# Vision-tower kernel: the tokenizer's last group in a hand-written order, and keys and values with their transposes one group ahead

## The chip, the cores and the metric

The kernel runs on one core of one Trainium2 chip. The metric is the device time of one launch in microseconds, as the median of several runs. A core has a matrix engine (TensorE, PE in the profile; its weight loads are shown as PEld), a vector engine (VectorE, DVE), a scalar engine (ScalarE, ACT), GpSimd (POOL) and a queue engine that issues transfers (SyncE, SP). Each engine works through its own list of instructions in order and waits for the others through semaphores.

## The reference

A small vision tower on four images of 3 x 224 x 224, all in 32-bit floats. The part that matters here is the tokenizer and the beginning of the attention of layer 0:

```
patches = 8 x 8 patches of x, 784 rows of 192 for each image
tokens  = layernorm(layernorm(patches) @ W1 + b1)
tokens  = concatenate([tokens, tokens, tokens], axis=1)
h       = silu(layernorm(tokens @ Wp1 + bp1)) @ Wp2 + bp2
# layer 0
m   = layernorm(layernorm(h) , gamma, beta)
q, k, v = m @ Wq, m @ Wk, m @ Wv
att = softmax over the images t of sum(q[s] * k[t]) per head
h   = h + (att applied to v, gated by sigmoid(m @ Wg + bg)) @ Wo + bo
h   = h + mixture of six experts, two for each row
# layer 1: linear attention, then a shared MLP and four experts, two for each row
```

The three copies of the tokens are equal, so the kernel computes one of them and writes each output row three times.

## The kernel before, in words

The 3136 rows (four images of 784) are cut into 28 tiles of 112 rows, and these into **seven groups of four tiles** (`groups`, `GT = 4`, `GN = 448` rows). The array `h` stays in SBUF for the whole kernel.

The tokenizer works by groups. For group g, `first_rows` (L506) multiplies the patches by a combined weight into PSUM (`pw`, L515), takes mean and variance of one half on VectorE (L519, L520), adds a correction (L522), takes a square root on ScalarE (L523) and its reciprocal on VectorE (L524). It then scales the other half (L528), takes its statistics (L531, L532), a second square root (L534) and reciprocal (L535), and writes the normalised rows `xn` (L538). `turned_rows` (L544) transposes `xn` on TensorE (in the helper `transposed`, L264) and applies Silu on ScalarE (L548) into `xTt`. The last part of `tokenize` (L566) multiplies `xTt` by `Wp2` (`pwp`, in the helper `mm_rows`, L284) and adds the bias into `h`. `tokenize(g)` does the first part for group g, the second for g - 1 and the third for g - 2. Up to the seventh group (g = 6) the planner of the framework decides how these instructions are interleaved on each engine.

From there on the order is written out by hand: inside `tc.manual_schedule` TensorE, VectorE and ScalarE execute in the order in which the program names the instructions. `tokenize(7)` and `tokenize(8)`, the leftovers of groups 5 and 6, stand in this part.

For keys and values, `second_norm(g)` takes the statistics of `h` (L236, L237) and works out the scale of two layer norms in a row, with two square roots on ScalarE (L239, L245). `second_rows(g)` writes the rows (L1060). `keys_values(g)` (L1065) transposes them, scales them on ScalarE into `mT` (L1070), multiplies by `Wk` and `Wv` (`pkv`, L273) and copies the products to `kq` and `vT` (L1079); in between it does `second_norm` and `second_rows` of group g + 1. At last it adds `bo` to `h` (L1087). After some of the groups come the products of queries and keys on VectorE (`products`, L739), and the first product with `headmask` (`pl`, L746) begins the attention proper.

Silu and square root need different function tables on ScalarE; a change from one to the other is an instruction of its own (ACT_TABLE_LOAD).

SP meanwhile fills two DRAM arrays, `xrows` and `yrows`, with zeros from the tile `nothing` (L468 to L473), in blocks of eight times 128 rows. Rows are scattered into `xrows` by GpSimd later (L950).

Of the kernel before, what the change touches and what calls it, by code (L numbers as in the profile page):

```python
# [27 lines left out]
P = 128  # L28
TT = 112
# [31 lines left out]
def tile_vit_tower(ctx: ExitStack, tc: tile.TileContext, a: dict, out: bass.AP):  # L61
# [168 lines left out]
    def ln_stats(src, n, twice=False):  # L230


        st = small.tile([TT, GT, 6], F32, tag="st", name="st")
        mv = small.tile([TT, GT, 2], F32, tag="mv", name="mv")
        for j in range(n):
            nc.vector.bn_stats(st[:, j, :], src(j))  # L236
            nc.vector.bn_aggr(mv[:, j, :], st[:, j, :])  # L237
        r = small.tile([TT, GT], F32, tag="rstd", name="rstd")
        nc.scalar.activation(r[:, :n], mv[:, :n, 1], AF.Sqrt, bias=eps[:TT])  # L239
        nc.vector.reciprocal(r[:, :n], r[:, :n])  # L240
        if twice:
# [27 lines left out]
    def mm_t(n, w, wcols, xT, name, chunks=2):  # L269

        pm = ps_tile(name)
        for c in range(chunks):
            nc.tensor.matmul(  # L273
                pm[: wcols.stop - wcols.start, :n], w[:, c, wcols], xT(c),
                start=(c == 0), stop=(c == chunks - 1),
            )
        return pm[: wcols.stop - wcols.start, :n]

    def mm_rows(tiles, xT, w, name, chunks=2):

        pm = ps_tile(name)[:TT].rearrange("p (t d) -> p t d", t=2)
        for i, t in enumerate(tiles):
            for c in range(chunks):
                nc.tensor.matmul(  # L284
                    pm[:, i, :], xT(c, t), w[:, c, :], start=(c == 0), stop=(c == chunks - 1)
                )
# [10 lines left out]
    def cut(t0, n):  # L297
        return slice(t0 * TT, (t0 + n) * TT)
# [166 lines left out]
        nc.tensor.transpose(pc[:, :nrows], stage, ident[:nrows, :nrows])  # L465
        turned = nc.vector.tensor_copy(cols, pc[:, :nrows])

    nothing = tokp.tile([P, 8 * D], F32, tag="nothing", name="nothing")  # L468
    nc.gpsimd.memset(nothing, 0.0)
    for r in range(0, XROWS, 8 * P):  # L470
        n = min(8, (XROWS - r) // P)
        for rows_ in (xrows, yrows):
            put = nc.sync.dma_start(  # L473
                out=rows_[r : r + n * P, :].rearrange("(p k) d -> p (k d)", k=n),
                in_=nothing[:, : n * D],
            )
# [27 lines left out]


    def first_rows(g):  # L506

        t0 = groups[g][0]
        y = tokp.tile([TT, GT, D], F32, tag="y", name="y", bufs=2)
        st = small.tile([TT, GT, 6], F32, tag="st", name="st")  # L510
        mv = small.tile([TT, GT, 2], F32, tag="mv", name="mv")
        for j in range(GT):
            pm = ps_tile("pw1")[:TT]
            for c in range(2):
                nc.tensor.matmul(  # L515
                    pm, pTf[:, c, cut(t0 + j, 1)], Wall[:, c, :], start=(c == 0), stop=(c == 1)
                )
# [5 lines left out]
        nc.scalar.activation(r, r, AF.Sqrt, bias=zero[:TT])  # L523
# [12 lines left out]
        xn = tokw.tile([TT, GT, D], F32, tag="xn", name="xn")  # L536
        for j in range(GT):
            nc.vector.tensor_scalar(  # L538
                xn[:, j, :], y[:, j, :], mv[:, j, 0:1], r[:, j : j + 1],
                ALU.subtract, ALU.mult,  # L540
            )
        return xn

    def turned_rows(xn):  # L544
        xT = tokw.tile([P, 2, GN], F32, tag="xTt", name="xTt")
# [10 lines left out]

    def tokenize(g):
        if g < len(groups):
            normed[g] = first_rows(g)
        if 1 <= g <= len(groups):  # L560
            third[g - 1] = turned_rows(normed.pop(g - 1))
        if g >= 2:
            sT = third.pop(g - 2)
            t2 = groups[g - 2][0]
            for two in halves(range(GT)):
                nc.vector.tensor_tensor(  # L566
                    h[:, t2 + two[0] : t2 + two[0] + 2, :],
                    mm_rows(two, lambda c, j: sT[:, c, cut(j, 1)], Wp2, "pwp2"),
                    over(bp2, 2), ALU.add,
                )  # L570
# [120 lines left out]
    ENG = mybir.EngineType  # L691
    by_hand = {ENG.DVE, ENG.PE, ENG.Activation}
    qTs, gates, atts, oTs, sums, rows0, turned0, logits0, picked, mixed = ({} for _ in range(10))
    pqs, pgs = {}, {}
    scatters = []
# [350 lines left out]
        nc.vector.tensor_tensor(wk[:, 1, t0 : t0 + n], second, first, ALU.mult)  # L1046


    xns = {}

    def second_norm(g):
        t0 = groups[g][0]
        return ln_stats(lambda j: h[:, t0 + j, :], GT, twice=True)

    def second_rows(g, stats):
        mv, r = stats
        t0 = groups[g][0]
        xn = xns[g] = tokw.tile([TT, GT, D], F32, tag="xn", name="xn")
        for j in range(GT):
            nc.vector.tensor_scalar(  # L1060
                xn[:, j, :], h[:, t0 + j, :], mv[:, j, 0:1], r[:, j : j + 1],
                ALU.subtract, ALU.mult,
            )

    def keys_values(g):  # L1065
        t0 = groups[g][0]
        at = cut(t0, GT)

        def put(c, pt):
            nc.scalar.activation(  # L1070
                mT[:, c, at], pt, AF.Identity, scale=col("gamma", c), bias=col("beta", c)
            )

        transposed(xns.pop(g), GT, put)
        if g + 1 < len(groups):
            stats = second_norm(g + 1)
        for w, dst in ((Wk, kT), (Wv, vT)):
            for o in range(2):
                nc.scalar.copy(  # L1079
                    dst[:, o, at],  # L1080
                    mm_t(GN, w, slice(o * P, (o + 1) * P), lambda c: mT[:, c, at], "pkv"),
                )
            if dst is kT and g + 1 < len(groups):
                second_rows(g + 1, stats)

        ht = h[:, t0 : t0 + GT, :]
# [816 lines left out]
```

## Time and profile before

| what | us |
|---|---|
| median of three runs | 787.35 (786.73 to 787.98) |
| the profiled execution, its own time | 833.42 |
| its span in the trace | 831.6 |
| TensorE busy in it | 744.5 |
| VectorE busy in it | 501.5 |
| ScalarE busy in it | 333.6 |
| GpSimd busy in it | 130.7 |

The profiled execution took longer than the runs without a profile. Durations below are from the profiled execution; differences are taken against its time, and carried over to the median. In the profile L12 is line 12 of the kernel, `out<-in` names the tiles, and `x8` counts instruction records; a 32-bit matrix product leaves two records. Ends of TensorE's records are modelled, so its starts are the better guide.

### The profile page before, as it was taken

What the parts mean: (1) busy time and instruction counts of PE and PEld (TensorE: products, weight loads), DVE (VectorE), ACT (ScalarE), POOL (GpSimd) and SP (SyncE); (2) the same over time, 40 slices, a digit from 0 to 9 for tenths busy, and PEclk for the clock granted to TensorE, in tenths of its full rate; (3) what the DMA queues carried; (4) which work ended last, traced back from release to release, by engine and by line L of the source; (5) the groups of instructions that cost most, each with busy time, mean ns of one, the idle gap of its engine ahead of it and who ended that gap; (6) DMA issues with size and microseconds to landing.
All of it is one profiled execution on the core that took longest, in us unless ns stands there. A gap on an engine that the chain in (4) does not pass through costs nothing.

```text
span 831.6 us, 10856 instructions
## 1 busy us (share of the span) xinstructions
PE 744.5 (90%) x3516; PEld 502.6 (60%) x3516; DVE 501.5 (60%) x1549; ACT 333.6 (40%) x789; POOL 130.7 (16%) x219
## 2 busy tenths in 40 slices
PE   7899969998987886999999997179999999999996
PEld 4655545555654564888878873155777685555553
DVE  4677775867878724355447565269994735555441
ACT  1567763556375732342223325114564503222221
POOL 5200000000256155300020206532000000000000
PEclk9999989999899888899999998669999999999998
DMA  8499994000012933232342342211000002333333
GB/s 208 147 420 417 421 418 206 1 2 0 20 59 62 368 93 117 86 113 88 96 128 89 112 125 86 78 45 33 2 1 0 1 4 64 95 96 99 95 99 92
DMA packets 58182, 97.38 MB, mean 117 GB/s; under 512 B 14519, under 2 KB 48494, under 8 KB 53262
## 3 DMA queue, kind: packets, MB, share of 16 engines
q1 hardware_dynamic: 50832, 80.52, 28.0%
q0 software_dynamic: 6112, 14.01, 5.8%
q10 hardware_dynamic: 1182, 2.16, 1.0%
q8 instruction: 28, 0.46, 0.2%
q14 instruction: 28, 0.23, 0.1%
HBM read 30.93 MB, written 65.74 MB: 116 GB/s over the span
## 4 chain that ended last, share of the span: by engine, by line
PE 73%; DVE 9%; ACT 6%; another core or an unknown queue 4%; issue 3%; DMA 2%; SPq 1%; POOL 0%; DVEq 0%; ACTq 0%; POOLq 0%
PE pb L1224 11%; PE pw L515 6%; PE pyb L1241 5%; PE pkv L273 5%; PE pe L273 5%; PE pqk L1625 4%; PE ps L273 4%; PE pt L264 3%; PE pwp L284 3%; PE pout L1740 3%; PE pout L1745 3%; PE ps L1857 3%; PE pukx L1699 3%; PE ps L1851 2%
## 5 line engine op out<-in xcount | busy, mean ns | idle before, releaser
L950 POOL DMA_INDIRECT xrows<-xn,pos x56 | 59.1, 1055 | 260.1 <-ACT kq L714 207.3
L1420 POOL DMA_INDIRECT ys<-yrows,pos x56 | 53.9, 962 | 167.0 <-DMA yrows<-yb 135.2
L1224 PE MATMUL pb<-xTb,own 128*128 128x256 f32 x240 | 60.7, 398 | 6.5 <-ACT xTb L1214 3.6
L1241 PE MATMUL pyb<-own,hb 128*128 128x256 f32 x240 | 58.4, 386 | 2.7 <-ACT hb L1230 2.4
L1230 ACT ACTIVATE hb<-pb,own 128x256 f32<-128x256 f32 x74 | 34.8, 475 | 63.0 <-PE pb L1224 42.0
L1224 PE MATMUL pb<-hb,own 128*128 128x256 f32 x240 | 58.7, 387 | 0.3 <-DVE hb L1232 0.3
L1224 PEld LDWEIGHTS pb<-xTb,own 128*128 128x128 f32 x240 | 45.6, 199 | 16.2 <-ACT xTb L1214 4.4
L1247 DVE TENSOR_TENSOR yb<-pyb,eb 128x512 f32<-128x512 f32 x30 | 20.7, 691 | 55.2 <-PE pyb L1241 39.3
L1241 PEld LDWEIGHTS pyb<-own,hb 128*128 128x128 f32 x240 | 45.8, 192 | 10.1 <-ACT hb L1230 3.2
L1625 PE MATMUL pqk<-Wqkv,lxT 128*112 128x512 f32 x112 | 50.0, 595 | 0.7 <-issue 0.5
L515 PE MATMUL pw<-Wall,pT 128*112 128x512 f32 x112 | 49.3, 593 | 0.0
L1224 PEld LDWEIGHTS pb<-hb,own 128*128 128x128 f32 x240 | 44.4, 195 | 6.7 <-DVE hb L1232 0.9
L1699 PE MATMUL pukx<-xa,uk 112*128 112x258 f32 x112 | 29.2, 418 | 18.1 <-ACT uk L1657 18.1
L1214 ACT COPY xTb<-ptb 128x512 f32<-128x512 f32 x30 | 17.5, 584 | 69.0 <-PE ptb L1210 63.7
L273 PE MATMUL pe<-xT,eW 128*128 128x448 f32 x112 | 45.2, 546 | 0.0
L264 PE MATMUL pt<-ident,xn 112*128 112x112 f32 x224 | 34.3, 286 | 11.5 <-DVE xn L538 6.6
L264 PEld LDWEIGHTS pt<-ident,xn 112*128 112x128 f32 x224 | 26.9, 151 | 25.6 <-issue 8.8
L1232 DVE TENSOR_SCALAR hb<-pb,own 128x256 f32<-128x256 f32 x46 | 22.1, 481 | 31.4 <-PE pb L1224 28.8
L1699 PEld LDWEIGHTS pukx<-xa,uk 112*128 112x128 f32 x112 | 22.9, 210 | 22.0 <-issue 18.4
L515 PEld LDWEIGHTS pw<-Wall,pT 128*112 128x112 f32 x112 | 19.6, 177 | 25.1 <-issue 21.4
L739 DVE SCALAR_TENSOR_TENSOR prod<-kq 128x784 f32<-128x784 f32 x32 | 30.3, 969 | 7.1 <-ACT kq L714 5.2
L1625 PEld LDWEIGHTS pqk<-Wqkv,lxT 128*112 128x112 f32 x112 | 19.2, 177 | 25.3 <-issue 24.2
(361 smaller groups left out, 1503.6 us busy)
## 6 DMA issues: line engine op xcount, KB each, us to landing
xrows<-nothing SPq DMA_DIRECT2D x19, 1024.0 KB, 19.6
yrows<-nothing SPq DMA_DIRECT2D x19, 1024.0 KB
out_dram<-h SPq DMA_DIRECT2D x26, 336.0 KB, 3.7
xb<-xrows SPq DMA_DIRECT2D x30, 256.0 KB, 2.8
yrows<-yb SPq DMA_DIRECT2D x30, 256.0 KB, 2.1
ew<-in_L_ffn_expert_w_dram SPq DMA_DIRECT2D x6, 768.0 KB, 11.8
wb<-wd SPq DMA_DIRECT2D x28, 112.0 KB, 3.3
img<-in_x_dram SPq DMA_DIRECT2D x2, 588.0 KB
```

The costliest lines, as they stand in the source:

```text
L264: nc.tensor.transpose(pt[:, j * TT : (j + 1) * TT], xn[:, j, c * P : (c + 1) * P], ident[:TT, :TT])
L273: nc.tensor.matmul(pm[: wcols.stop - wcols.start, :n], w[:, c, wcols], xT(c), start=(c == 0), stop=(c == chunks - 1),)
L284: nc.tensor.matmul(pm[:, i, :], xT(c, t), w[:, c, :], start=(c == 0), stop=(c == chunks - 1))
L515: nc.tensor.matmul(pm, pTf[:, c, cut(t0 + j, 1)], Wall[:, c, :], start=(c == 0), stop=(c == 1))
L739: nc.vector.scalar_tensor_tensor(prod, qTs[s][:, o, :], 1.0, kT[:, o, t * SEQ : (t + 1) * SEQ], ALU.mult, ALU.mult, accum_out=atts[s][:, o ...
L950: put = nc.gpsimd.indirect_dma_start(out=xrows[:, :], out_offset=bass.IndirectOffsetOnAxis(ap=pos[:, k, t0 + j : t0 + j + 1], axis=0), in_ ...
L1224: nc.tensor.matmul(pm, wm[:, c, o * P : (o + 1) * P], src[:, c, :], start=(c == 0), stop=(c == 1),)
L1230: nc.scalar.activation(dst[:, o, :], pm, AF.Relu, bias=b)
L1241: nc.tensor.matmul(pm[:, t, :], src[:, c, t * P : (t + 1) * P], wm[:, c, :], start=(c == 0), stop=(c == 1),)
L1420: got = nc.gpsimd.indirect_dma_start(out=y[:, j, k, :], out_offset=None, in_=yrows[:, :], in_offset=bass.IndirectOffsetOnAxis(ap=pos[:, k, ...
L1625: nc.tensor.matmul(pqk, xT[:, c, cut(j, 1)], Wqkv[:, c, : 2 * D], start=(c == 0), stop=(c == 1),)
L1699: nc.tensor.matmul(pg, uks[u][:, k, c * P : (c + 1) * P], xas[u % 4][:, k, : D + 2], start=(j == 0), stop=(j == TPI - 1),)
```

## The change

1. `first_rows` becomes the generator `first_steps`, with a stop after the first reciprocal and another after the second statistics.
2. The planner's loop covers only groups 0 to 5. Before the last of these, `second_norm(0)` and `second_rows(0)` are done, so the rows of the first keys group are ready early. `xn` gets a third buffer (`bufs=3`) for that.
3. Group 6 is in a hand-written block. Its first step comes before the Silu of group 5; then come the transposes and Silu of group 5, the second step, `last_rows(4)`, and the rest.
4. Keys and values are split. `turn_second(g)` does the transposes and `mT`, `projected` one of the two products with its copies. `keys_values(g)` does the product with `Wk`, the statistics of group g + 2, the transposes of group g + 1, the product with `Wv`, and the rows of group g + 2. In group 0 the transposes and Silu of group 6 stand ahead of those of group 1, and `last_rows(6)` after the product with `Wv`.
5. `nothing` holds seven rows of 256 for each partition in place of eight, so the zeros go out in 46 transfers in place of 40.

```diff
-    nothing = tokp.tile([P, 8 * D], F32, tag="nothing", name="nothing")
+    nothing = tokp.tile([P, 7 * D], F32, tag="nothing", name="nothing")
     nc.gpsimd.memset(nothing, 0.0)
-    for r in range(0, XROWS, 8 * P):
-        n = min(8, (XROWS - r) // P)
+    for r in range(0, XROWS, 7 * P):
+        n = min(7, (XROWS - r) // P)
...
     def first_rows(g):
+        for _ in first_steps(g):
+            pass
+
+    def first_steps(g):
...
         nc.scalar.activation(r, r, AF.Sqrt, bias=zero[:TT])
         nc.vector.reciprocal(r, r)
+        yield
...
             nc.vector.bn_aggr(mv[:, j, :], st[:, j, :])
+        yield
         r = small.tile([TT, GT], F32, tag="rstd", name="rstd")
...
-        xn = tokw.tile([TT, GT, D], F32, tag="xn", name="xn")
+        xn = tokw.tile([TT, GT, D], F32, tag="xn", name="xn", bufs=3)
...
-        return xn
+        normed[g] = xn
...
-    for g in range(len(groups)):
+    n = len(groups)
+    for g in range(n - 1):
+        if g == n - 2:
+            second_rows(0, second_norm(0))
         tokenize(g)
+    ENG = mybir.EngineType
+    by_hand = {ENG.DVE, ENG.PE, ENG.Activation}
+    with tc.manual_schedule(engines=by_hand):
+        steps = first_steps(n - 1)
+        next(steps)
+        third[n - 2] = turned_rows(normed.pop(n - 2))
+        next(steps)
+        last_rows(n - 3)
+        for _ in steps:
+            pass
     tok.close()
...
+    def turn_second(g):
+        if g >= len(groups):
+            return
+        at = cut(groups[g][0], GT)
...
         transposed(xns.pop(g), GT, put)
-        if g + 1 < len(groups):
-            stats = second_norm(g + 1)
-        for w, dst in ((Wk, kT), (Wv, vT)):
-            for o in range(2):
-                nc.scalar.copy(
-                    dst[:, o, at],
-                    mm_t(GN, w, slice(o * P, (o + 1) * P), lambda c: mT[:, c, at], "pkv"),
-                )
-            if dst is kT and g + 1 < len(groups):
-                second_rows(g + 1, stats)
...
+    def keys_values(g):
+        projected(g, Wk, kT)
+        if g + 2 < len(groups):
+            stats = second_norm(g + 2)
+        if g == 0:
+            third[n - 1] = turned_rows(normed.pop(n - 1))
+        turn_second(g + 1)
+        projected(g, Wv, vT)
+        if g == 0:
+            last_rows(n - 1)
+        if g + 2 < len(groups):
+            second_rows(g + 2, stats)
...
     with tc.manual_schedule(engines=by_hand):
-        second_rows(0, second_norm(0))
-        tokenize(len(groups))
+        turn_second(0)
+        last_rows(n - 2)
+        second_rows(1, second_norm(1))
         keys_values(0)
-        tokenize(len(groups) + 1)
         for g in range(1, len(groups)):
             keys_values(g)
```

More of the change, by code (lines that the diff above doesn't have):

```diff
@@ L558, in tokenize @@
         if g < len(groups):
-            normed[g] = first_rows(g)
+            first_rows(g)
         if 1 <= g <= len(groups):
@@ L562, in tokenize, with last_rows, second_norm, second_rows @@
         if g >= 2:
[L563 to L569, printed above, removed]
-                )
-    for g in range(len(groups)):
-        tokenize(g)
+            last_rows(g - 2)
+    def last_rows(g):
+        sT = third.pop(g)
+        t2 = groups[g][0]
+        for two in halves(range(GT)):
+            nc.vector.tensor_tensor(
+                h[:, t2 + two[0] : t2 + two[0] + 2, :],
+                mm_rows(two, lambda c, j: sT[:, c, cut(j, 1)], Wp2, "pwp2"),
+                over(bp2, 2), ALU.add,
+            )
+    xns = {}
+    def second_norm(g):
+        t0 = groups[g][0]
+        return ln_stats(lambda j: h[:, t0 + j, :], GT, twice=True)
+    def second_rows(g, stats):
+        mv, r = stats
+        t0 = groups[g][0]
+        xn = xns[g] = tokw.tile([TT, GT, D], F32, tag="xn", name="xn", bufs=3)
+        for j in range(GT):
+            nc.vector.tensor_scalar(
+                xn[:, j, :], h[:, t0 + j, :], mv[:, j, 0:1], r[:, j : j + 1],
+                ALU.subtract, ALU.mult,
+            )
+    n = len(groups)
+    for g in range(n - 1):
+        if g == n - 2:
+            second_rows(0, second_norm(0))
+        tokenize(g)
+    ENG = mybir.EngineType
[8 more added lines that the diff above has]
+            pass
     tok.close()
@@ L690, in tile_vit_tower @@
     nc.vector.tensor_scalar(bgh, col2("bg"), 0.5, None, ALU.mult)
-    ENG = mybir.EngineType
-    by_hand = {ENG.DVE, ENG.PE, ENG.Activation}
     qTs, gates, atts, oTs, sums, rows0, turned0, logits0, picked, mixed = ({} for _ in range(10))
@@ L1046, in mix3 @@
         nc.vector.tensor_tensor(wk[:, 1, t0 : t0 + n], second, first, ALU.mult)
[L1049 to L1067, printed above, removed]
+    def turn_second(g):
+        if g >= len(groups):
+            return
+        at = cut(groups[g][0], GT)
         def put(c, pt):
@@ L1074, in keys_values, with projected @@
         transposed(xns.pop(g), GT, put)
-        if g + 1 < len(groups):
-            stats = second_norm(g + 1)
-        for w, dst in ((Wk, kT), (Wv, vT)):
-            for o in range(2):
-                nc.scalar.copy(
-                    dst[:, o, at],
-                    mm_t(GN, w, slice(o * P, (o + 1) * P), lambda c: mT[:, c, at], "pkv"),
-                )
-            if dst is kT and g + 1 < len(groups):
-                second_rows(g + 1, stats)
-        ht = h[:, t0 : t0 + GT, :]
+    def projected(g, w, dst):
+        at = cut(groups[g][0], GT)
+        for o in range(2):
+            nc.scalar.copy(
+                dst[:, o, at],
+                mm_t(GN, w, slice(o * P, (o + 1) * P), lambda c: mT[:, c, at], "pkv"),
+            )
+    def keys_values(g):
[10 more added lines that the diff above has]
+            second_rows(g + 2, stats)
+        ht = h[:, groups[g][0] : groups[g][0] + GT, :]
         nc.vector.tensor_tensor(ht, ht, over(bo, GT), ALU.add)
     with tc.manual_schedule(engines=by_hand):
-        second_rows(0, second_norm(0))
-        tokenize(len(groups))
+        turn_second(0)
+        last_rows(n - 2)
+        second_rows(1, second_norm(1))
         keys_values(0)
-        tokenize(len(groups) + 1)
         for g in range(1, len(groups)):
```

## The prediction

> **What bounds the kernel now.** I read the page's busy shares, then the TensorE timeline over 94 to 182 us (the stretch that the edits touch), then the granted clock in narrow windows, then VectorE's and ScalarE's timelines across the one long hole.
>
> ```profile
> PE 744.5 (90%) x3516; PEld 502.6 (60%) x3516; DVE 501.5 (60%) x1549; ACT 333.6 (40%) x789; POOL 130.7 (16%) x219
> ```
>
> TensorE is the bound over the whole, so microseconds in which it waits or runs slowly are what an edit can win. Its timeline (start, us, what; idle time and releaser in brackets):
>
> ```profile
> 93.86 7.03 PE L515 MATMUL pw<-Wall,pT 128*112 128x512 f32 x16
> ...
> 105.05 0.32 PE L577 MATMUL ptable<-ident,table 1*78 1x1 f32 x4
> 111.94 2.07 PE L264 MATMUL pt<-ident,xn 112*128 112x112 f32 x8 [6.57 <-DVE xn L538]
> 113.80 5.33 PE L284 MATMUL pwp<-Wp,xTt 128*112 128x256 f32 x16
> 118.97 0.93 PE L264 MATMUL pt<-ident,xn 112*128 112x112 f32 x8
> 120.33 3.27 PE L273 MATMUL pkv<-mT,Wk 128*128 128x448 f32 x8 [0.43 <-ACT mT L1070]
> 123.44 3.17 PE L273 MATMUL pkv<-mT,Wv 128*128 128x448 f32 x8
> 126.45 3.62 PE L284 MATMUL pwp<-Wp,xTt 128*112 128x256 f32 x16
> ```
>
> After the seventh group's products L515 TensorE runs dry for 6.57 us, waiting for that group's normalised rows (xn, L538). Then the same eight transposes take 2.07 us instead of 0.93, and the same sixteen records of pwp 5.33 instead of 3.62. The windows say why (PEclk is the last column but two):
>
> ```profile
> 105.00:110.00 5.00, 0.37 (x5) 0.23 (x4) 4.84 (x18) 4.19 (x6) 0.00 (x0) 1.00 1.01 419
> 110.00:112.00 2.00, 0.06 (x1) 0.09 (x1) 1.86 (x9) 0.30 (x1) 0.00 (x0) 0.61 1.02 418
> 112.00:114.00 2.00, 2.00 (x9) 1.64 (x10) 1.51 (x8) 0.71 (x2) 0.00 (x0) 0.50 1.04 426
> 114.00:116.00 2.00, 2.00 (x7) 1.42 (x6) 1.38 (x4) 1.99 (x3) 0.00 (x0) 0.50 1.01 414
> 116.00:118.00 2.00, 2.00 (x8) 1.53 (x7) 0.56 (x1) 0.23 (x1) 0.00 (x0) 0.69 1.01 410
> ```
>
> The clock halves at about 110.4 and is back at about 117.2. Why are the rows late? ScalarE stands between:
>
> ```profile
> 103.28 0.72 ACT L548 ACTIVATE xTt<-pt,cols 128x448 f32<-128x448 f32 x1
> 104.03 1.28 ACT L523 ACT_TABLE_LOAD   x1
> 105.32 0.30 ACT L523 ACTIVATE rstd<-rstd,zero 112x4 f32<-112x4 f32 x1
> ```
>
> The square root L523 had its input from VectorE at 102.19 (L522, 102.03 plus 0.16) but stood behind another group's Silu and its table; VectorE's reciprocal L524 came only at 105.77. Later VectorE ran the first keys group's statistics (L236, 109.09 to 111.2) ahead of the reciprocal L535 that the seventh group needs.
>
> [...] The trace agrees: halved 5.0 us after the work stopped at 105.37, restored 5.3 us after it resumed at 111.94. It also shows a harder case: at 206.0 us the clock fell (0.50 over 206.0 to 209.4) though no single wait before it was over 0.99 us; sparse transposes were enough. [...] the trace shows 1.28 us with the square root at once behind it, so I price a switch at 1.28.
>
> **The change, part by part.** W2(g) below is last_rows (pwp), T(g) a group's eight transposes (0.93 us), groups 0 to 6.
>
> *What can be won in this stretch.* The hole 6.57. The seven waits for mT before each Wk product: three of 0.43 and four of 0.48, together 3.21. The cold clock: 2.07 − 0.93 = 1.1 and 5.33 − 3.62 = 1.7, together 2.8. Sum 12.6 us. Matrix products are only reordered, so this is the ceiling.
>
> *Last group by hand, and turned later.* The order is now products L515 of group 6, T(5), W2(4), the table, T(0), W2(5), Wk(0), and only then T(6). Between the products and T(6) lie 0.93 + 3.45 + 0.3 + 0.93 + 3.45 + 3.1 = 12.2 us of TensorE work, where 4.6 us stood before (100.73 to 105.37). The rows came 11.2 us after the products (100.73 to 111.94), so T(6) should not wait. (W2 is 126.45 to 129.90, Wk 120.33 to 123.44, each from start to the next start.) The square root goes ahead of the Silu of T(5), and saves that Silu's tables: the built program has 37 table loads for 39. ScalarE's two loads fewer (2.6 us) are off TensorE's path and priced at nothing beyond the hole.
>
> *second_norm(0) and second_rows(0) moved up, ahead of group 5.* About 3.6 us more for VectorE in a cycle of 11.1 (four statistics with aggregates at 0.42, small steps 0.6, rows 1.3) in which it was idle 2.8 (1.24 + 1.04 + 0.51). It comes out 0.8 late, and since the hand order no longer interleaves, TensorE waits for xn(5) ahead of T(5): bound 0 to 2.5, I take 1.5. Rows arriving 0.34 apart spread the transposes by another 0.7. **A: 2.2 lost.**
>
> *T(1) behind Wk(0).* From the end of W2(5), VectorE must add h (0.75), do the statistics to the rows (130.71 to 134.64 in the trace of group 2: 3.93), and give the first row (0.5): 5.2; TensorE has Wk 3.1 and T(6) 0.93. Wait 1.2, plus 0.4 for xn(6) queued ahead of that add, plus 0.7 of spread. Bounds 0 to 4. **B: 2.3 lost.**
>
> *W2(6) behind Wv(0).* It needs the Silu of T(6). ScalarE holds that behind both square roots of second_norm(2), which VectorE begins only after xn(1). From xn(1)'s first row: other rows 1.0, to the second root 3.19 (130.71 to 133.90), root 0.3, table 1.28, first Silu 0.72, hand-over 0.1: 6.6. TensorE has T(1) 1.6 and Wv 3.1. Bounds 0.5 to 3.5. **C: 1.9 lost.** The mT and vT copies queued behind the Silu fall into later slack.
>
> *Transposes one group ahead.* T(g+1) runs between Wk and Wv, so mT's 1.34 us on ScalarE lies under 3.1 us of Wv: six of the seven waits go, and the first too (T(0) runs before W2(5)). If that cover were gone, 0.45 each would return. VectorE was 77% busy over 140 to 160 (15.39 of 20); with the group's period cut from 7.53 to about 6.9 it becomes 84%, not yet the bound. Allow **D: 0.2**, bounds 0 to 1.5.
>
> *Zeros in blocks of seven.* 46 transfers for 40, the same bytes at 419 GB/s; six more issues at 0.33 us on SP, which waits on landings there anyway. The transfers end near 135, scatters start after 220: nothing, bounds 0 to 0.3. The first kq copy waits for the kernel's first loads in both built programs, not for the zeros still under way then. A third buffer for xn adds no wait.
>
> *Clock afterwards.* A and B are each a wait followed by sparse transposes, like the case at 206.0. [...] After B it mostly falls on Wv and eats wait C, free; after A it costs up to 1.7. Mean 1.0, bounds 0 to 3.4.
>
> **Sum.** 12.6 − (2.2 + 2.3 + 1.9 + 0.2) − 1.0 = **5.0 us** won by the first pl (L746, 180.26). Beyond it all waits are on work of the chain itself, so I pass it on whole. The profiled execution took 833.42 (span 831.6), 46 above the median of 787.35; the chain shows waits of 6.10, 4.88 and 11.09 us on unknown queues at 516 to 540, far from this stretch, so I take 5.0 off the median: **782.3**.
>
> **Rivals.**
> 1. *Smaller gain*: A, B and C nearer their upper bounds and two cold spells. 12.6 − 8 − 2.5 = 2.1: 785.2. For it: the manual order forbids filling a gap with other work.
> 2. *Nothing*: VectorE becomes the bound of the keys; six periods of 6.9 us stretch back to 7.5 (3.6) and B and C grow by 1.4 together: 5.0 − 5.0 = 0, 787.4. Against it: 77% busy.
> 3. *Slower*: the clock stays at half from A through C[...]. Loss is half the cold time. With 6.6 of waits, it decides against the change from (12.6 − 6.6) × 2 = 12 us cold; the stretch from A to W2(6)'s end, some 25 us, would cost 12.5 and give 793.8. Against it: W2(5) with Wk(0) is about 7 us dense, enough for recovery by the trace's 5.3.
> 4. *Not what it says*: the built program shows all moves above, so this is excluded.
>
> **How the numbers follow.** 0.2% is 1.6 us, about what measurement of this kernel can tell from no change. Main case 0.64 (gain 3.4 to 7), rival 1 0.19 (gain 1.6 to 3.4), within 0.2% 0.07, slower 0.10. Faster is 0.83. The likeliest case's range is 780.3 to 784.0; for 8 in 10, with most of rival 1, 779.8 to 786.2.
>
> **What would show it.** Right: no TensorE wait over 2.5 us between 95 and 130; waits of 1 to 2 us ahead of T(5), T(1) and W2(6); no mT wait before Wk; the first pl near 175; clock not at 0.5 for over 7 us. Wrong: a wait on xn(6) at T(6), one over 3 us anywhere, or a cold clock throughout 103 to 128.

## The result and the profile after

The changed kernel took **781.75 us** (median of 4 runs, 780.17 to 781.97) where the kernel before, on the same chip, took 787.29 (4 runs, 786.73 to 787.98): ratio 0.9925, 95% interval 0.9908 to 0.9942, so 5.5 us faster by the medians, and 4.6 to 7.2 by the interval. The forecast was 782.3, range 779.8 to 786.2.

The profiled execution took 781.84 us (span 780.1). The page's busy shares:

```profile
PE 732.4 (94%) x3516; PEld 495.7 (64%) x3516; DVE 500.2 (64%) x1549; ACT 330.5 (42%) x787; POOL 134.4 (17%) x219
```

The execution profiled before took 833.42, far above the 787 of the other runs; profiling isn't the reason, since the one profiled after lies among its runs (780.17 to 781.97), and on the chips of the experiments the kernel before takes 827. TensorE's share rose from 90% to 94%, but most of that is not the change: from the first pl to the end of the span the execution profiled before took 651.3 us and this one 604.9, in code that no edit touches. The wait list over 480 to 580 of the experiment e5 below, which runs the changed kernel on another chip (engine, tile, line, releaser: us in total, times, longest), has the largest of those losses too:

```profile
POOL ys L1455 <- DMA yrows<-yb: 21.9, 1, 21.9
...
PE pukx L1734 <- ACT uk L1692: 18.4, 1, 18.4
```

The profile after shows neither, the profile before shows both (21.8 and 18.1), so it goes with the chip or the execution, not with the kernel; which of the two isn't shown. The two spans must not be subtracted; only the stretch that was edited can be compared. TensorE's timeline of it, after (start, us, what; idle time and releaser in brackets):

```profile
96.36 7.03 PE L519 MATMUL pw<-Wall,pT 128*112 128x512 f32 x16
104.50 1.58 PE L264 MATMUL pt<-ident,xn 112*128 112x112 f32 x8 [1.11 <-DVE xn L544]
...
113.98 3.17 PE L273 MATMUL pkv<-mT,Wk 128*128 128x448 f32 x8
116.99 0.93 PE L264 MATMUL pt<-ident,xn 112*128 112x112 f32 x8
119.65 1.57 PE L264 MATMUL pt<-ident,xn 112*128 112x112 f32 x8 [1.73 <-DVE xn L593]
121.06 4.88 PE L273 MATMUL pkv<-mT,Wv 128*128 128x448 f32 x8
125.96 3.89 PE L284 MATMUL pwp<-Wp,xTt 128*112 128x256 f32 x16
129.69 3.17 PE L273 MATMUL pkv<-mT,Wk 128*128 128x448 f32 x8
132.70 0.93 PE L264 MATMUL pt<-ident,xn 112*128 112x112 f32 x8
133.47 3.19 PE L273 MATMUL pkv<-mT,Wv 128*128 128x448 f32 x8
...
175.22 0.28 PE L784 MATMUL pl<-part,headmask 128*128 128x8 f32 x2
```

The hole of 6.57 us is gone, and the last group's transposes (116.99) follow Wk without a wait. Two waits stand in its place, 1.11 ahead of the sixth group's transposes and 1.73 ahead of the second keys group's. The mT waits are gone: Wk follows pwp, and Wv follows the next group's transposes 0.77 us after their start (132.70 to 133.47). One product is long, Wv at 121.06: 4.88 us for 3.19. The narrow windows (the last columns are the granted clock, the DMA share and GB/s) say why:

```profile
120.00:122.00 2.00, 1.99 (x9) 1.21 (x10) 1.90 (x9) 0.00 (x0) 0.00 (x0) 0.87 1.02 423
122.00:124.00 2.00, 2.00 (x4) 1.01 (x3) 1.17 (x7) 0.71 (x3) 0.00 (x0) 0.50 0.99 409
124.00:126.00 2.00, 1.98 (x5) 0.57 (x3) 0.24 (x2) 1.99 (x3) 0.00 (x0) 0.78 1.05 434
```

The clock is at half (0.50) from about 121.5 to 124.9, 3.4 us, where before it was so for 6.8. ScalarE's timeline shows what Silu of the last group stands behind:

```profile
106.11 0.30 ACT L527 ACTIVATE rstd<-rstd,zero 112x4 f32<-112x4 f32 x1 [2.16 <-DVE rstd L526]
...
107.72 1.34 ACT L554 ACTIVATE xTt<-pt,cols 128x448 f32<-128x448 f32 x2
...
123.57 0.30 ACT L245 ACTIVATE v<-v,eps 112x4 f32<-112x4 f32 x1 [0.64 <-DVE v L244]
...
125.19 1.34 ACT L554 ACTIVATE xTt<-pt,cols 128x448 f32<-128x448 f32 x2
```

The square root L527 now runs as soon as its input is there; the load of Silu's table (1.28 us) and the sixth group's Silu come behind it. The last group's Silu (125.19) runs only after a root of the third keys group (L245, 123.57), and pwp at 125.96 follows it. The wait ahead of that root (0.64) is for VectorE.

**The measure used below.** The totals scatter: on the three chips of the experiments, before took 827.2, 827.1 and 827.5 us with single times from 822 to 834. A trace of the stretch is sharper. I take the time from the start of the fifth group's products (the first record of its sixteen, L515 or L519) to the first pl. Three traces with the stretch as before give 108.6, 108.1 and 107.7 (before, e1 and e11; mean 108.1), by how much of pwp the half clock covers (in before it read 0.50 from 110.4 to 117.3, and pwp starts at 113.80; pwp takes 5.17, 4.61 and 4.25 us from start to start); the changed kernel gives 101.4 in both of its traces (73.84 to 175.22 after, 72.63 to 174.02 in e5). So the stretch won **6.7 us** against the mean, and 7.2 against the one trace of before that the prediction used.

| kernel | stretch, us | less than 108.1 | total, median us | ratio to before, 95% |
|---|---|---|---|---|
| e1 before again | 108.1 | | 830.5 (one run) | |
| e2 keys alone | 105.6 | 2.5 | 822.75 | 0.9953 (0.9927 to 0.9979) |
| e3 tokenizer alone | 102.0 | 6.1 | 818.21 | 0.9895 (0.9864 to 0.9925) |
| e4 Silu first | 105.5 | 2.6 | 823.44 | 0.9956 (0.9933 to 0.9978) |
| e5 the change | 101.4 | 6.7 | 818.42 | 0.9898 (0.9865 to 0.9932) |
| e6 hole kept warm | 106.4 | 1.7 | 822.06 | 0.9942 (0.9920 to 0.9965) |
| e7 both hand-overs | 98.2 | 9.9 | 815.81 | 0.9862 (0.9821 to 0.9904) |
| e8 both, early statistics | 96.4 | 11.7 | 813.05 | 0.9827 (0.9795 to 0.9859) |
| e9 Silu ahead | 100.9 | 7.2 | 820.34 | 0.9904 (0.9866 to 0.9942) |
| e10 Wv ahead | 104.0 | 4.1 | 823.36 | 0.9945 (0.9922 to 0.9967) |
| e11 zeros in sevens | 107.7 | | 830.34 | 1.0025 (1.0001 to 1.0048) |
| e12 roots last | 96.5 | 11.6 | 816.85 | 0.9866 (0.9819 to 0.9913) |

e1 to e4, e5 to e8 and e9 to e12 ran together, each group on one chip. The medians of e2, e4 and e10 include one slow run each (831.72, 2617.04 and 830.73 us, the second for a reason that isn't known), which the ratios leave out.

### The profile page after: what moved, and what is told of

The parts are those of the page before. It is cut to its first block, busy times and chain, and to the rows that moved or that the text cites. A ratio compares the mean times of both kernels' runs of the same rounds, so it can differ in the third digit from the quotient of the medians.

```text
span 780.1 us, 10857 instructions
## 1 busy us (share of the span) xinstructions
PE 732.4 (94%) x3516; PEld 495.7 (64%) x3516; DVE 500.2 (64%) x1549; ACT 330.5 (42%) x787; POOL 134.4 (17%) x219
## 5 line engine op out<-in xcount | busy, mean ns | idle before, releaser
L1455 POOL DMA_INDIRECT ys<-yrows,pos x56 | 56.2, 1004 | 143.2 <-DMA yrows<-yb 127.1
L1259 PE MATMUL pb<-hb,own 128*128 128x256 f32 x240 | 57.1, 380 | 0.3 <-DVE hb L1267 0.3
L519 PE MATMUL pw<-Wall,pT 128*112 128x512 f32 x112 | 49.3, 593 | 0.0
L519 PEld LDWEIGHTS pw<-Wall,pT 128*112 128x112 f32 x112 | 19.6, 177 | 25.1 <-issue 21.7
L1668 ACT ACTIVATE qk<-qk 112x256 f32<-112x256 f32 x56 | 22.8, 407 | 27.6 <-DVE qk L1664 25.1
L273 PEld LDWEIGHTS pe<-xT,eW 128*128 128x128 f32 x112 | 20.2, 190 | 20.9 <-issue 20.7
```

Of the source, the lines that this page charges most:

```text
L273: nc.tensor.matmul(pm[: wcols.stop - wcols.start, :n], w[:, c, wcols], xT(c), start=(c == 0), stop=(c == chunks - 1),)
L519: nc.tensor.matmul(pm, pTf[:, c, cut(t0 + j, 1)], Wall[:, c, :], start=(c == 0), stop=(c == 1))
L1259: nc.tensor.matmul(pm, wm[:, c, o * P : (o + 1) * P], src[:, c, :], start=(c == 0), stop=(c == 1),)
L1455: got = nc.gpsimd.indirect_dma_start(out=y[:, j, k, :], out_offset=None, in_=yrows[:, :], in_offset=bass.IndirectOffsetOnAxis(ap=pos[:, k, ...
```

## The experiments

The diffs of e2, e3, e4 and e7 are against the changed kernel (so e2 to e4 keep the zeros in sevens), those of e6 and e11 against the kernel before, of e8 against e7 and of e12 against e8. T(g) and last_rows are named as in the prediction.

**e1, the kernel before as it is** (no edit), to see what of its trace repeats.

> The kernel before, unchanged, profiled once more. My account: the hole ahead of the seventh group's transposes is again 6 to 7 us, the clock halves again inside or just after it (1 to 3 us lost, by where it falls), and the seven waits before the Wk products are there. The cold spell at 22 to 29 us that only the changed kernel's profile showed is chance: it may or may not show here, and costs about 2 us where it does. Rival (the changed kernel starts later for a reason of its own): here the first products L515 start within 0.3 us of 34.7 again.

Measured: 830.49 us, the stretch 108.1; the hole and a clock at half for 6.8 us from 110.1 are there again, and the first products start at 35.46 for 34.65, later than the 0.3 us of the rival. The cold spell at 22 to 29 us isn't there. So the hole is the kernel's, not that execution's.

**e2, the keys as a pipeline, the tokenizer's last group left to the scheduler.** The keys' pipeline stays, the fixed order goes:

```
-    for g in range(n - 1):
-        if g == n - 2:
-            second_rows(0, second_norm(0))
+    for g in range(n):
         tokenize(g)
...
-    with tc.manual_schedule(engines=by_hand):
-        steps = first_steps(n - 1)
...
-        if g == 0:
-            third[n - 1] = turned_rows(normed.pop(n - 1))
...
     with tc.manual_schedule(engines=by_hand):
+        second_rows(0, second_norm(0))
+        tokenize(n)
         turn_second(0)
-        last_rows(n - 2)
```

> Only the keys' part of the change: transposes one group ahead, the zeros in blocks of seven, but the tokenizer's last group and its order as before. My account (the tokenizer's part brings most): the hole of 6.6 us and the cold clock stay, the waits before Wk go (4.3 by start-to-start times), but new waits on VectorE's rows stand in the first keys group: 0.5 to 2 us faster than before. Rival (the pipeline of the keys brings most): 4 to 5.5 us faster.

Measured: 3.9 us by the ratio (1.7 to 6.0), 2.5 in the stretch; between my account and the rival. The hole is as it was, the first mT wait stays and T(1) now waits. TensorE in e2:

```profile
121.69 3.27 PE L273 MATMUL pkv<-mT,Wk 128*128 128x448 f32 x8 [0.43 <-ACT mT L1084]
125.80 1.58 PE L264 MATMUL pt<-ident,xn 112*128 112x112 f32 x8 [0.84 <-DVE xn L593]
```

It won more than my account allowed because the new wait is small: T(1) starts 1.00 us after Wk's 3.11 and spreads by 0.64, 1.6 us in all. And a mT wait is worth more than the idle time in its record. Before, Wk starts 1.36 us after the start of the transposes with a wait of 0.43 shown (118.97 to 120.33), and 1.41 with 0.48 (157.67 to 159.08); in the changed kernel Wv starts 0.77 after them. Each hand-over is 0.59 or 0.64, not 0.43 or 0.48, and Wk behind it takes 3.11 to the next start (120.33 to 123.44), without it 3.01 (129.69 to 132.70 after).

**e3, the tokenizer's last group in the fixed order, the keys as before** (each group turned right ahead of its Wk):

```
     def keys_values(g):
+        if g:
+            turn_second(g)
+        if g + 1 < len(groups):
+            stats = second_norm(g + 1)
         projected(g, Wk, kT)
-        if g + 2 < len(groups):
-            stats = second_norm(g + 2)
...
-        turn_second(g + 1)
+        if g + 1 < len(groups):
+            second_rows(g + 1, stats)
         projected(g, Wv, vT)
...
```

> Only the tokenizer's part: last group by hand, first keys rows early, its transposes behind Wk of the first keys group; the keys turn each group right before its own Wk product, as before. My account: the hole and most of the cold clock go, wait B (rows of the second keys group) goes too since those transposes come later, six waits of about 0.6 return: 4 to 6 us faster than before, so about as fast as the whole change. Rival (the keys bring most): 0 to 2 us faster.

Measured: 8.7 by the ratio (6.2 to 11.2), 6.1 in the stretch, at or above the upper end. The fixed order carries nearly all of the change's 6.7; e2 and e3 sum to 8.6, so the two parts don't add up. Here T(1) comes after Wv, so the wait ahead of it doesn't exist, and the last group's Silu stands behind the roots of one keys group, not of two: in e3 pwp waits 0.76 for it and takes no longer than in e7 (3.89), where the clock read 1.00. TensorE in e3:

```profile
121.31 3.89 PE L284 MATMUL pwp<-Wp,xTt 128*112 128x256 f32 x16 [0.76 <-ACT xTt L554]
```

The pipeline, put on top, removes six mT hand-overs (about 4.3 us with the longer Wk behind each) and brings T(1)'s wait and what follows it.

**e4, the whole change with the last group's Silu ahead of the square root:** turned_rows of the sixth group is issued ahead of L527 in place of behind it (`ahead` is the line removed below).

```
+        if ahead:
+            ahead()
         yield
...
-        third[n - 2] = turned_rows(normed.pop(n - 2))
...
```

> The whole change, but in the last group ScalarE does the Silu of group 5 ahead of the group's first square root. My account: the rows of group 6 have 3.7 us of slack, so TensorE does not wait for them; but VectorE's list stands still behind the reciprocal for about 2.6 us (table 1.28, two Silus 1.34), and rows of the second keys group come that much later, so wait B grows: 2 to 2.8 us slower than the whole change, 2.5 to 3.5 faster than before. Rival (the order of square root and Silu is off the path): within 0.5 us of the whole change.

Measured: 2.6 less than before in the stretch, 4.1 more than the change; by the ratio 3.6 faster than before. The gain on before is in the range; the loss against the change was too low, and it lies elsewhere than I said: wait B did not grow, it fell from 1.73 to 1.20. ScalarE, then TensorE in e4:

```profile
106.06 1.34 ACT L559 ACTIVATE xTt<-pt,cols 128x448 f32<-128x448 f32 x2
...
108.72 0.30 ACT L532 ACTIVATE rstd<-rstd,zero 112x4 f32<-112x4 f32 x1
114.74 0.30 ACT L545 ACTIVATE rstd<-mv,eps 112x4 f32<-112x4 f32 x1 [5.72 <-DVE mv L542]
```
```profile
115.71 3.27 PE L273 MATMUL pkv<-mT,Wk 128*128 128x448 f32 x8 [2.56 <-ACT mT L1098]
...
120.95 1.67 PE L264 MATMUL pt<-ident,xn 112*128 112x112 f32 x8 [1.20 <-DVE xn L598]
...
127.36 5.58 PE L284 MATMUL pwp<-Wp,xTt 128*112 128x256 f32 x16 [1.72 <-ACT xTt L559]
```

The root runs 13.4 us after the start of the seventh group's products (95.34), in e5 9.75 after it (104.90, with 95.15). VectorE comes late by that, and with it the group's second root (L545), behind which mT of the first keys group stands on ScalarE: Wk waits 2.56 for it. Another 1.7 us come from a slow pwp (5.4 us from its start to the next, for 3.7); that a cold clock slows it is my estimate from e10, where pwp took 6.36 with the clock at 0.50 to 0.52.

**e5, the changed kernel again**, on the chip of e6 to e8.

> The changed kernel as it is, on the chip of the next three runs, to compare them with. If the stretch up to the first pl carries the gain on every chip: 4.5 to 7.5 us faster than before (ratio 0.990 to 0.994). If a later stage gives part of it back or adds to it by the chip: outside these.

Measured: 8.4 us faster by the ratio, 5.6 to 11.2, and the same 101.4 in the stretch. The middle lies 0.9 above the upper end that was expected and the interval reaches well below it, so the totals don't tell whether a later stage adds something; the stretch repeats to the hundredth (101.38 and 101.39).

**e6, before with the hole kept warm**: unused products ahead of the last group's transposes.

```
+        for _ in range(14):
+            idle = ps_tile("pidle")
+            nc.tensor.matmul(idle[:, :D], ident, Wk[:, 0, :], start=True, stop=True)
```

> The kernel before, with 14 products of the identity with Wk (128x256, about 3 us of TensorE by pwp's 0.215 us each) put into the hole of 6.57 us, their results unused. The price of the cold clock by itself. If the prediction's term stands (1.1 us on the transposes, 1.7 on pwp): with a warm clock the transposes of the last group still have to follow rows that come 0.34 us apart (about 1.5 us for 2.07), so 1.7 to 2.8 us faster than before, the hole shorter by the filling, the transposes' start unmoved at about 18.1 us behind the start of the seventh group's products. If VectorE and ScalarE hold what follows (rival): within 0.5 us of before though the clock reads 1.00.

Measured: 1.7 less in the stretch, 4.8 by the ratio (2.9 to 6.6). TensorE in e6:

```profile
106.38 6.31 PE L1092 MATMUL pidle<-Wk,ident 128*128 128x256 f32 x28
113.02 1.58 PE L264 MATMUL pt<-ident,xn 112*128 112x112 f32 x8 [0.33 <-DVE xn L538]
114.43 3.62 PE L284 MATMUL pwp<-Wp,xTt 128*112 128x256 f32 x16
```

The 14 products ran as 28 records, twice my estimate, and filled the hole. The clock read 1.00 throughout 100 to 130. The transposes start 18.07 us after the products of the seventh group (94.95), before 18.08: the cold clock doesn't move that start, the rows (xn L538) do. What comes after is shorter: transposes 1.41 for 1.86 from start to start, pwp 3.46 for 5.17. That is 2.2 us against the profile of before; the prediction's 2.8 counted transposes of 0.93, but with the rows 0.34 apart they don't get below 1.41. The cold clock was 2.2, the hole 6.57. The larger gain of the totals isn't explained by the stretch; single times ran from 818.9 to 830.1, and the trace is from the slowest of them.

**e7, two hand-overs turned round**, in keys_values, for the first group:

```
         projected(g, Wk, kT)
-        if g + 2 < len(groups):
-            stats = second_norm(g + 2)
         if g == 0:
             third[n - 1] = turned_rows(normed.pop(n - 1))
-        turn_second(g + 1)
-        projected(g, Wv, vT)
+        if g + 2 < len(groups):
+            stats = second_norm(g + 2)
         if g == 0:
+            projected(g, Wv, vT)
+            turn_second(g + 1)
             last_rows(n - 1)
+        else:
+            turn_second(g + 1)
+            projected(g, Wv, vT)
```

(the later groups keep the change's order)

> The changed kernel with two hand-overs of the first keys groups put the other way: the Silu of the last group is issued ahead of the third keys group's statistics and square roots (wait C), and in the first keys group the Wv product goes ahead of the second group's transposes (wait B). If waits B and C are what the prediction says they are (2.3 and 1.9 us, of which the spread of the transposes, 0.6, is covered too): 2.5 to 4 us faster than the changed kernel, and TensorE shows no wait over 0.6 us from the first Wk product to the third. If the waits move on instead (VectorE's chain for the second keys group still ends late, and Wk of the second group waits for mT in its place): 0 to 1.5 us faster than the changed kernel.

Measured: the stretch 3.2 shorter than the change's, the median 2.6. TensorE in e7:

```profile
117.59 3.19 PE L273 MATMUL pkv<-mT,Wv 128*128 128x448 f32 x8
120.61 0.93 PE L264 MATMUL pt<-ident,xn 112*128 112x112 f32 x8
121.53 3.89 PE L284 MATMUL pwp<-Wp,xTt 128*112 128x256 f32 x16
126.17 3.27 PE L273 MATMUL pkv<-mT,Wk 128*128 128x448 f32 x8 [0.75 <-ACT mT L1094]
```

No wait from Wk to pwp, Wv back at 3.02 from start to start, the clock 1.00 throughout. Only a wait of 0.75 for mT ahead of the second Wk is over the 0.6 that I allowed.

**e8, e7 with the first keys group's statistics one tokenizer cycle earlier:**

```
     for g in range(n - 1):
+        if g == n - 3:
+            stats0 = second_norm(0)
         if g == n - 2:
-            second_rows(0, second_norm(0))
+            second_rows(0, stats0)
```

> The run before this one, and besides the statistics of the first keys group issued one tokenizer cycle earlier, with the rows left where they are (wait A). If wait A is VectorE's extra work in the cycle of the sixth group (2.2 us): 1.5 to 3.5 us faster than the run before this one, so 4.5 to 6.5 us faster than the changed kernel, and the sixth group's transposes follow the products with under 0.5 us of idle. If the extra work is only moved one cycle (VectorE is as full there): within 0.7 us of the run before this one, and a wait of about 1 us ahead of the fifth group's transposes.

Measured: 1.8 less in the stretch than e7 (98.2 to 96.4), 2.8 by the medians. TensorE in e8:

```profile
105.69 0.97 PE L264 MATMUL pt<-ident,xn 112*128 112x112 f32 x8
```

The products start at 98.82 and last 6.87, so the sixth group's transposes follow them directly, as expected, and take 0.80 to the next start for 1.41. The rows of the first keys group (L593) moved with the statistics, though the program names them in the same place. VectorE in the change, then in e8:

```profile
97.85 1.38 DVE L593 TENSOR_SCALAR xn<-h,mv,rstd 112x256 f32<-112x256 f32 x4
```
```profile
94.88 1.37 DVE L593 TENSOR_SCALAR xn<-h,mv,rstd 112x256 f32<-112x256 f32 x4
```

In the change they stand among the steps of the sixth group, behind its reciprocal L528 (97.25); in e8 they stand ahead of it (100.12). So T(5) seems to wait for these 1.38 us rather than for the statistics; no run moves the rows alone. The 0.3 us that the change lost one cycle earlier is now lost yet a cycle earlier (the sixth group's products start 11.42 after the fifth's, not 11.10). **e8 is the fastest version:** 14.1 us less than before by the medians (ratio 0.9827) and 5.4 less than the change, on the same chip.

**e9, the Silu's half of e7**: turned_rows of the last group ahead of second_norm of the third keys group, T(1) still ahead of Wv.

> One half of the run with both: the changed kernel with only the Silu of the last group ahead of the third keys group's statistics (wait C alone). Measured from the start of the seventh group's products to the first pl; the changed kernel has 78.9 us there, the one with both 75.6. If C is a loss by itself: 1.5 to 2 us less than 78.9. If C only covered the slow clock of the Wv product (4.9 us for 3.0), which stays since wait B stays: 0 to 0.7 us less, and the Wv product at a clock of 0.5 is then followed by pwp with no wait.

**e10, Wv's half of e7**: Wv ahead of T(1), the Silu still behind the roots.

> The other half: the changed kernel with only the first Wv product ahead of the second group's transposes (wait B alone). Same measure. If the waits B and C add up: 2 to 2.5 us less than 78.9. If both hang on one chain (VectorE's rows of the second group, then the square roots of the third, then the Silu of the last group on ScalarE), moving TensorE's work only moves its wait to the place ahead of pwp: between 0.5 us less and 1.5 us more than 78.9.

Measured from the seventh group's products to the first pl, where the change has 78.9: e9 78.4, so 0.4 less; e10 81.5, so 2.6 more. TensorE in e9, and its windows:

```profile
119.61 4.71 PE L273 MATMUL pkv<-mT,Wv 128*128 128x448 f32 x8
124.15 3.62 PE L284 MATMUL pwp<-Wp,xTt 128*112 128x256 f32 x16
```
```profile
120.00:122.00 2.00, 2.00 (x4) 0.80 (x3) 0.91 (x4) 1.97 (x4) 0.00 (x0) 0.50 1.02 419
```

The Silu is early, nothing waits for it, and Wv still takes 4.54 from start to start at a clock of 0.50. TensorE in e10, and its windows:

```profile
125.17 6.52 PE L284 MATMUL pwp<-Wp,xTt 128*112 128x256 f32 x16 [4.25 <-ACT xTt L554]
```
```profile
124.00:126.00 2.00, 0.83 (x2) 0.66 (x3) 0.00 (x0) 1.99 (x4) 0.00 (x0) 0.52 1.01 419
```

Wv is done at full clock (1.00 over 114 to 120), but pwp waits 4.25 us for the Silu, and the clock falls on pwp (0.52 above, then 0.50 over 126 to 130). It starts 29.61 us after the seventh group's products (125.17 less 95.56); in the change 29.60 (125.96 less 96.36), in e5 29.60. Where Wv stands makes no difference to that: VectorE's rows of the second group, the third group's statistics and roots, the table and the Silu make up one chain that ends there. So B and C are not two losses. In the change the wait ahead of T(1), its sparse transposes and the cold Wv all lie in time that this chain takes anyway. Taking only the Silu out leaves the cold Wv; taking only Wv out uncovers the chain; both together win 3.2. That e10 lost 2.6 where I allowed 1.5 is the cold clock: pwp takes 6.36 from start to start for 3.73, which is the whole 2.6.

**e11, the zeros in blocks of seven, alone:**

```
-    nothing = tokp.tile([P, 8 * D], F32, tag="nothing", name="nothing")
+    nothing = tokp.tile([P, 7 * D], F32, tag="nothing", name="nothing")
...
-    for r in range(0, XROWS, 8 * P):
+    for r in range(0, XROWS, 7 * P):
```

> The kernel before with the one edit of the change that touches no computation: the zeros written in 46 transfers of seven blocks for 40 of eight. If it costs nothing, as forecast: same as before within the interval, from the seventh group's products to the first pl 85.9 to 86.4 us as before. If SP or the queues were in the way: over 1 us slower, and the patches' first products later than 34.7 to 36.8 us.

Measured: nothing in the stretch (107.7; 85.5 from the seventh group's products, where pwp lost less to the cold clock than in before and e1, 4.25 us for 5.17 and 4.61), the first products at 36.61, inside the band that I gave and behind a cold spell (a clock of 0.50 over 24 to 28; last section), but a median 2.8 us higher and a ratio of 1.0025 with an interval just clear of 1. Beside that spell the trace shows no place for it up to the first pl. A cost of this edit of up to some 4 us is thus neither shown nor excluded.

**e12, e8 with the third group's statistics and roots behind the second group's turned rows:**

```
-        if g + 2 < len(groups):
+        if g + 2 < len(groups) and g > 0:
             stats = second_norm(g + 2)
         if g == 0:
             projected(g, Wv, vT)
             turn_second(g + 1)
+            stats = second_norm(g + 2)
```

> The fastest version so far (both hand-overs and the early statistics), with the third keys group's statistics and square roots issued behind the second group's turned rows, so that mT of the second group no longer stands on ScalarE behind them. From the start of the sixth group's products to the first pl that version had 84.95 us. If the last wait there (0.75 us shown ahead of the second Wk, 1.2 from start to start) is only that order: 0.8 to 1.2 us less. If the third group's rows then come late: a wait of about 1 us ahead of its transposes in place of the one removed, and within 0.3 us of 84.95.

Measured: the rival. From the sixth group's products 85.1 for e8's 84.95. TensorE in e12:

```profile
125.90 1.66 PE L264 MATMUL pt<-ident,xn 112*128 112x112 f32 x8 [0.29 <-DVE xn L593]
```

The wait for mT is gone, and one for the third group's rows has come ahead of its transposes, which also spread to 1.50 from start to start.

## Why the prediction was right, point by point

**What could be won.** The hole went whole: 6.57. The mT waits were under-sized, the sum's largest miss: 3.21 taken from the idle shown, 4.33 from start to start (three of 0.59 and four of 0.64), and 0.7 more because Wk behind each of the seven takes 3.11 for 3.01: 5.0 in all. The cold clock's 2.8 is confirmed as time that went, though e6 shows that 0.6 of it was the spacing of the last group's rows and not the clock. Both go in the change, where the rows are there early. The ceiling was thus about 14.4, not 12.6.

**A, 2.2 predicted.** Measured 2.2: a wait of 1.27 (the products' 6.87 end at 103.23, T(5) starts at 104.50), 0.64 of spread (1.41 for 0.77) and 0.33 one cycle earlier. e8 removes its cause, VectorE's work for the first keys group, and T(5) then follows at once. The prediction put all of this work into one cycle; in the trace the statistics cost the 0.33 a cycle earlier, and it is the rows that stand among the sixth group's steps.

**B, 2.3 predicted.** Measured 2.5: T(1) starts 2.66 us after T(6) for 0.77 (116.99 to 119.65), which is 1.9, and 0.64 of spread.

**C, 1.9, and the new cold clock, 1.0.** Together 2.9 predicted, the 1.0 an estimate; measured 2.2 (pwp starts 4.90 after Wv for 3.02, and takes 3.73 for 3.45). That the cold clock after B would fall on Wv and cost nothing held: it lasted 3.4 us there (0.50 over 122 to 124), and C shows no idle time since the slow product fills it, so that of the three waits forecast only two can be seen. That B and C add up as losses in themselves fell: e9 and e10 show one chain. The sum came out because each was computed with the other present; as advice on what to mend it was wrong.

**D, 0.2.** Measured 0.3 (in e5 one Wv of 3.18 from start to start for 3.02, 157.92 to 161.10, and the Wk behind it of 3.12 for 3.01). The group's period went from 7.53 to 6.80.

**The sum.** 14.4 less 2.2, 2.5, 2.2 and 0.3 is 7.2, which is what the stretch won against the trace of before that these figures come from (108.6 to 101.4); the prediction had 5.0. Of the 2.2 between, 1.8 is the mT waits and 0.7 the clock with C, less 0.2 for B and 0.1 for D. That the median moved by 5.5, so near to 5.0, is in part luck. "The first pl near 175" was met at 175.22 by two errors that cancelled: the stretch won 7.2 for 5.0, and this execution started its first products 2.2 us late (36.82 for 34.65), where the clock read 0.50 over 24 to 28 and lower than full on both sides (0.81 and 0.84). Over the same 4 us it read 0.50 in e10 and e11, 0.58 in e5 and 0.61 in e8 and e9, all with the zeros in sevens, and 1.00 in before and e6, with eights, so the zeros are a suspect; but in e7 and e12, in sevens, it read 1.00 too, and e5, the same kernel as this one, has 3.4 us of the spell for 6.8 here and starts at 35.60. The last section sets five of these traces beside their other falls.

**What reached the end.** 5.5 (4.6 to 7.2) on the first chip and 8.4 (5.6 to 11.2) on that of e5; 6.7 lies within both. How much of it is kept on the first chip, and whether e11's cost takes part of it back, the runs can't tell.

**The rivals.** *Smaller gain*: A, B and C stayed at their middles. *Nothing*: VectorE was busy 15.96 of 20 us at 140 to 160, 80%, and TensorE 20.00 of 20. *Slower*: there was one cold spell, and pwp with Wk stood between A and B at full clock (1.00 over 104 to 117), as argued. The transposes of the last group did not wait, as forecast: their rows were written from 113.27 to 114.6, and they start at 116.99.

## What to carry to other kernels

Price a hand-over from start to start against the same pair where nothing waits, with the instruction behind it, not by the idle time in its record. Before counting two waits as two gains, look whether one chain of other engines ends behind both: if a step starts at the same distance from a common origin whatever TensorE does in between, only shortening that chain helps, and the waits ahead of it have to be mended together. And read a local edit in its own stretch of the trace when the total scatters by more than the edit is worth.

## What the runs showed of the hardware that I had not expected

The granted clock fell without a long wait: in the change the longest wait from 96.36 to the fall at 121.5 was 1.73 us, between transposes of 0.93 and 1.57 us. In the 3.41 us ahead of the fall TensorE was busy for 1.82 (118.07 to 121.48), in e5 for 1.66 (116.12 to 119.53). It fell 4.5 us after the last dense product there (Wk's end at 117.0, the fall near 121.5), and 3.7 after it in e5 (115.8 and 119.5, by the clock's mean of 0.88 over 118 to 120). The low spells in the edited stretch were 3.4 us long (after, e5, e9) or 6.8 (before, e1, e10, e11), nothing between.

The falls also lie at even distances. In before and after each low spell (but for the last, at 827.2 and 776.8, which the end of the trace cuts) lasts 3.4 us or a multiple of it: 3.4 or 6.8, and once, before from 526.9, 20.5. The falls of one trace lie whole steps of 3.41 us apart: after, the falls at 22.5 and 121.5 are 99.0 us or 29 steps apart; before, those at 110.4 and 206.0 are 95.6 or 28. By windows of 2 us over 180 to 540 the falls of e1 to e9 and of e11 do the same (e5: 201.4 and 232.2, 9 steps). So it may also depend on where a gap lies to these steps whether it costs clock. The cold spell at the start of the kernel would fit this. TensorE waits 2.18 to 2.29 us there in after, before, e9, e10 and e11 before it goes on with the patches' transposes. It goes on at 23.08 in after, 22.68 in e9, 22.57 in e10 and 22.63 in e11, and the clock falls 0.6 us before that, 1.0 after, 0.9 before and 0.9 before. In before, which has no spell there, it goes on at 22.68, and the steps counted back from its fall at 110.4 lie 1.0 us before that and 2.4 after. The nearest cases on the two sides are only 0.1 us apart, and no run tests it.

Cold spells may also explain part of the scatter. Windows 310 to 340 of e1 and then of e5, in the routing that the change doesn't touch (the clock is the last column but two):

```profile
310.00:340.00 30.00, 19.92 (x80) 16.42 (x80) 11.12 (x48) 6.53 (x14) 13.61 (x15) 0.77 0.35 107
```
```profile
310.00:340.00 30.00, 25.69 (x130) 21.46 (x131) 12.71 (x40) 10.42 (x22) 13.87 (x18) 0.94 0.37 108
```

By windows of 0.1 us the clock of before and after reads 1.00 or 0.50 except where it changes. I estimate from that: a clock of 0.77 over 30 us is 13.8 us at half, so at most about 7 us lost; 0.94 is 3.6 us at half, and at most 1.8 lost. It is less where TensorE waited anyway (it was busy for 19.92 and 25.69 of the 30), and the two windows don't hold quite the same work. These 5 us between two executions would be as much as the whole edit; whether an earlier start of this stage changes the number of its spells, or chance, stays open.
